# Four edits to a two-layer attention and convolution kernel: an engine for the edge corrections, a queue for two weights, the place of the next image's statistics, and the adder of one block

## The chip, the cores and the metric

The kernel runs on one core of a Trainium2 chip. The core has a matrix engine (TensorE, called PE in the profile), two engines for elementwise work (VectorE, DVE, and ScalarE, ACT), a general one (GpSimd, POOL) and an engine that only issues transfers (SyncE, SP). Each engine works through its own list of instructions in order; semaphores tie the lists together. Loads and stores are DMA transfers, issued by an instruction on SP, POOL or ACT and carried out by 16 DMA engines that all of them share. The metric is the time of the whole program in microseconds of device time; lower is better.

## The reference

The input x has two images of 256 channels and 64 x 64 positions, in fp32. Two layers are applied, each as x + layer(GroupNorm(x)), with 32 groups in the norm:

```python
# layer 0: 1x1 convolution to q, k, v; 8 heads of 32 channels; all 4096 positions
qkv = einsum('bchw,oc->bohw', gn(x), qkv_w) + qkv_b
x = x + einsum('bhij,bhcj->bhci', softmax(q_i . k_j / sqrt(32)), v)
# layer 1: three 1x1 convolutions of g = gn(x), a position term added to q and k
ctx   = attention over 64 positions, a position from each 8 x 8 block   ("lr")
feats = relu(scale * lr_W(ctx) + shift)
qx, kx = two 1x1 convolutions with scale, shift and relu each, of feats
ctx2  = attention over the 64 positions inside one block, v = sr_fv(feats) ("sr")
out_att  = relu(scale * sr_W(ctx2) + shift)
out_conv = 3x3 grouped convolution, padded by 1, of a mix of q, k and v
x = x + rate1 * out_att + rate2 * out_conv
```

Inside one image everything of layer 1 depends on the statistics of all of layer 0's result. The two images don't depend on each other.

## The kernel before, in words

`direct_layers` handles the images one after the other. x is kept in SBUF as eight tiles of 512 positions (128 partitions, two channel halves each); the pool of them (`xpool`, line 48) has nine places, so eight for an image and one more: a tile of the next image can be loaded when a tile of this one has been released by its last reader.

*Start.* SP's queue holds, in this order, 16 loads of 32 x 256 values into `w1_by_out` and `w2_by_out` (lines 79 to 88), which `fold_scores` (lines 186 to 225) multiplies into weights that layer 1 uses; two small tables; and the eight tiles of x (`load_x`, lines 66 to 74). POOL's queue has the weights of layer 0 (`load_layer0`, lines 120 to 131) and many small constants. `group_stats` (line 331) takes the statistics of x tile by tile on DVE, sums them over the channel groups by two small matmuls, `pm` and `pv`, copies between them on DVE, and ends in a square root on ACT, which needs another table of functions, and a reciprocal on DVE. Then `normalise` makes `xn`, and `project0` (line 392) makes keys (`p_wk`), queries (`p_wq`) and values, splits keys and queries into high and low halves and stores all of them to DRAM; the attention fetches them head by head.

*Layer 0.* `attention0` works on 16 groups `g` (8 heads, each with two halves of the queries) of 32 blocks `j` of 128 keys. A block has four units of 128 keys x 512 queries. PE makes scores in rounds of 3 + 2 + 2 units (`sa`, `sb`, `sc`, line 493), ACT takes the exponential of each (line 499) into a ring of 28 places, of which 17 lie in a tile `es` and 11 in a tile called `v` (`RING`, line 445), and PE multiplies them with the values (`av`, line 509), some rounds behind. The softmax also needs the sum of each row's exponentials, over all blocks. `add_rows` (line 524) makes it: DVE adds most blocks into a tile `e` (lines 538 to 546, two adds of 128 x 1024 a block), but the seven blocks of `SUMMED` (line 447) are summed by DMAs that POOL issues in `add_in_memory` (lines 548 to 556). The first of the seven, block 3, is copied into `acc` and `pair` (line 554); the other six are added there by accumulating DMAs (line 556). A place of the ring can be written again when both the matmuls and the adds have read it. In a group's first block after the last, DVE adds `acc` and `pair` to `e`, and a matmul with ones makes the row sums. The order of PE, ACT and DVE in this stage is written out by hand (`tc.manual_schedule`).

*Layer 1, first part.* `layer1_first` normalises into groups and runs the "lr" attention; its names end in `_lr`.

*Layer 1, second part.* `layer1_second` (line 1204) goes over eight tiles `t` of 512 positions. For each, PE runs the branches fq and fk (`branch`: matmuls `phq`, `prq`, `phk`, `prk`, with the relu on ACT into `hq`, `rq`, `hk`, `rk`), then `group_attention`, a generator that stops at each `yield`: values (`pvs`) and scores (`sp_sr`); transposes (`at_sr`) and, on DVE, copies into `bd` (line 1043); the products with the values (`pc_sr`, line 1052), which ACT turns into `res_sr` (line 1063). Beside that runs the convolution: POOL transforms the image (`conv_transform`, lines 911 and 915), PE multiplies (`conv_step`, `mm`, line 925) into the one accumulator of the pool `pacc`, ACT copies a part of it to `z`, DVE combines the rest and adds the result into x (lines 934 to 953). The transform is right inside the image; at its borders `conv_edges` (lines 954 to 971) adds or takes away a bias in single columns, rows and corners of x, 88 tiny instructions in all. In image 0, after tile 1, `conv_weights` makes the convolution's weights on DVE piece by piece and stores them; the load of `wf` brings them back and 64 transposes (`pw`, line 884) turn them. At the end of a tile, results that are complete are given out: two `scalar_tensor_tensor` on DVE make rate1 * res + x (line 1322), SP stores them, and with that the tile of x is free. In this part PE's order is written out by hand; the order of the other engines is set by the scheduler.

*Between the images.* The loop (lines 1330 to 1353) starts the next image by `load_x(1)`, `load_layer0(1)` and `group_stats`, after all of `layer1_second(0)`.

Of the kernel before, what the change touches and what calls it, by code (L numbers as in the profile page):

```python
# [12 lines left out]
AF = mybir.ActivationFunctionType  # L13
ALU = mybir.AluOpType
# [3 lines left out]
P = 128  # L18
B, C, H, W = 2, 256, 64, 64
N = H * W  # L20
T = 512
NT = N // T
KC = C // P
# [17 lines left out]
def direct_layers(ctx: ExitStack, tc: tile.TileContext, a: dict, out: bass.AP, bad: bass.AP):  # L41
# [24 lines left out]
    def load_x(b):  # L66
        tiles = []
        for t in range(NT):
            xt = xpool.tile([P, KC, T], F32, tag="x", name=f"x_{b}_{t}")
            nc.sync.dma_start(  # L70
                out=xt,
                in_=a["x"][b, :, t * T : (t + 1) * T].rearrange("(k p) n -> p k n", p=P),
            )
            tiles.append(xt)
        return tiles
# [4 lines left out]
    for name in ("w1", "w2"):  # L80
        by_out[name] = wpool.tile([P, KC, C], F32, tag="wp", name=f"{name}_by_out")

        for i in range(4):
            for half in range(2):
                r = 64 * (i % 2) + 32 * half
                nc.sync.dma_start(
                    out=by_out[name][r : r + 32, i // 2, :], in_=a["wx"][int(name == "w2"), half, i, 0:P:4, :]
                )
    place_rows = w4([4, C], "place_rows")
    nc.sync.dma_start(out=place_rows, in_=a["posq"])  # L90
    grid = const.tile([2, 64], F32, name="grid")
# [239 lines left out]
    def group_stats(xts, tagn):  # L331
        st = Stats(xts, tagn)
        for t in range(NT):
            for k in range(KC):
                st.tile(k, t)
        both, pv = slice(0, KC), bank([P, KC], f"pv_{tagn}")
        st.aggregate(both)
        st.means(both, bank([P, KC], f"pm_{tagn}"), nc.vector.tensor_copy)
        st.spread(both)
        st.variances(both, pv)  # L340
        st.deviations(both, pv)
        return st.mean, st.rstd
# [103 lines left out]

    SUMMED = (3, 7, 11, 15, 18, 22, 26)


    SUMMED_LAST = (NJ - 3, NJ - 2, NJ - 1)  # L450

    def attention0(b, xts, held):
# [71 lines left out]
        def add_rows(g, j):  # L524
            if j == 0:
                sums[g] = psum["sc"].tile([P, T], F32, tag="av", name=f"av_{b}_{g}")
                added[g] = [w4([P, 2, T], f"e_{b}_{g}_{w}") for w in range(2)]
                return
            for w in range(2):
                dst = added[g][w]  # L530
                if j in SUMMED:
                    if w == 0:
                        add_in_memory(g, j)
                    continue
                if j == 1:
                    first = two_units(g, 0, w), two_units(g, 1, w)
                    if len(first[0]) == len(first[1]) == 1:
                        nc.vector.tensor_add(dst, first[0][0][1], first[1][0][1])
                    else:
                        for s in range(2):  # L540
                            nc.vector.tensor_add(dst[:, s, :], unit(g, 0, 2 * w + s), unit(g, 1, 2 * w + s))
                    continue
                for s, src in two_units(g, j, w):
                    if g == last and j in SUMMED_LAST:
                        continue
                    nc.vector.tensor_add(dst[:, s, :], dst[:, s, :], src)  # L546

        def add_in_memory(g, j):
            assert not waiting or j != SUMMED[0]
            runs = [(acc[u].unsqueeze(1), unit(g, j, u).unsqueeze(1)) for u in (0, 1)]  # L550
            runs += [(pair[:, s, :], src) for s, src in two_units(g, j, 1)]
            for dst, src in runs:
                if j == SUMMED[0]:
                    nc.gpsimd.dma_start(out=dst, in_=src)
                else:
                    nc.gpsimd.dma_start(out=dst, in_=src, accum_op=ALU.add)  # L556
# [397 lines left out]
    def conv_edges(xts, t):  # L954

        btap, edges = kept["bias"]
        for m in range(2):
            def add(dst, what):
                nc.vector.tensor_scalar(dst, dst, what, None, ALU.add)

            x = xts[t][:, m, :]
            add(x[:, 0:T:W], edges[:, m, 3:4])
            add(x[:, W - 1 : T : W], edges[:, m, 4:5])
            if t == 0:
                add(x[:, 0:W], edges[:, m, 1:2])
                add(x[:, 0:1], btap[:, m, 0:1])
                add(x[:, W - 1 : W], btap[:, m, 2:3])
            if t == NT - 1:
                add(x[:, T - W : T], edges[:, m, 2:3])
                add(x[:, T - W : T - W + 1], btap[:, m, 6:7])  # L970
                add(x[:, T - 1 : T], btap[:, m, 8:9])
# [229 lines left out]
        kept["seam"] = done.ins  # L1201
        return feats, mean, rstd, shift

    def layer1_second(b, xts, feats, mean, rstd, shift, pacc):

        xp = apool.tile([P, KC, PADW, PADW], F32, tag="A", name=f"xp_{b}")
        for k in range(KC):
# [24 lines left out]
        def conv():  # L1232
            nonlocal done, wf
            if wf is None:
                wf = fetch_conv_weights(b)
            if done + 1 < len(turns):
                ahead[done + 1] = conv_transform(b, xp, *turns[done + 1])
            conv_step(b, xts, wf, ahead.pop(done), *turns[done], pacc)
            done += 1

        if b:
            for t in range(3):
# [3 lines left out]
        for t in range(NT):  # L1246
# [25 lines left out]
            with tc.manual_schedule(engines={mybir.EngineType.PE}):  # L1272
                q = branch("fq1", "fq2", V_FQ1, V_FQ2, "q")
                if pending:
                    next(pending)
                    next(pending, None)
                    pending = None
                for tt in images.get(t, ()):
                    to_image(tt)
                if 0 in spots.get(t, ()):  # L1280
                    conv()
                k = branch("fk1", "fk2", V_FK1, V_FK2, "k")
                res = w4([P, KC, T], f"res_{nt}")

                def to_res(m, pc, res=res):

                    bn_relu(
                        res[:, m, :].rearrange("p (d o e) -> p o d e", d=8, o=8),
                        pc.rearrange("p (o d e) -> p o d e", o=8, d=8), V_SRW, m,
                    )  # L1290

                parts = group_attention(
                    nt, q, k, lambda c, w, f=f: f[c][:, w * P : (w + 1) * P], wts["fv"], to_res, apart=t + 1 < NT
                )
                next(parts)
                if 1 in spots.get(t, ()):
                    conv()
                if t < 2 and b == 0:
                    pending = parts
                else:  # L1300
                    next(parts)
                    next(parts, None)
                if 2 in spots.get(t, ()):
                    conv()
# [12 lines left out]
                report()  # L1317
            results[t] = res
            for n in sorted(n for n in results if done >= 4 * (n // 2 + 1)):
                res = results.pop(n)  # L1320
                for m in range(KC):
                    nc.vector.scalar_tensor_tensor(  # L1322
                        res[:, m, :], res[:, m, :], wts["rate1"], xts[n][:, m, :], ALU.mult, ALU.add
                    )
                nc.sync.dma_start(
                    out=out[b, :, n * T : (n + 1) * T].rearrange("(k p) n -> p k n", p=P), in_=res
                )


    for b in range(B):  # L1330
        xts = x_first if b == 0 else load_x(b)
        w0 = w0_first if b == 0 else load_layer0(b)
        with tc.tile_pool(name=f"ps0_{b}", bufs=8, space=PSUM) as psum["ps"]:
            if b == 0:
                fold_scores()
            mean, rstd = group_stats(xts, f"l0_{b}")
            xn = apool.tile([P, KC, N], F32, tag="A", name=f"xn_{b}")
            for t in range(NT):
                for k in range(KC):
                    normalise(xn[:, k, t * T : (t + 1) * T], xts[t][:, k, :], k, mean, rstd)  # L1340
            held = project0(b, xn, w0)
        if b == 0:
            load_layer1()
        load_set(b, ("w3",) if b == 0 else ("g", "w3"))
        with tc.tile_pool(name=f"sc_{b}", bufs=1, space=PSUM) as psum["sc"]:
            put, check, st = attention0(b, xts, held)
        with tc.tile_pool(name=f"ps1_{b}", bufs=8, space=PSUM) as psum["ps"]:
            between = layer1_first(b, xts, put, check, st)
        with (
            tc.tile_pool(name=f"pacc_{b}", bufs=1, space=PSUM) as pacc,  # L1350
            tc.tile_pool(name=f"ps2_{b}", bufs=4, space=PSUM) as psum["ps"],
        ):
            layer1_second(b, xts, *between, pacc)


@with_exitstack
# [555 lines left out]
```

## Time and profile before

| | |
|---|---|
| median of 3 runs | 3140.06 us (3138.55 to 3142.82) |
| the profiled execution, its own time | 3143.21 us |
| its span, first to last instruction | 3141.1 us |
| mean granted clock of PE | 0.992 |

Span and busy time by stage, in us, as read from the trace:

| stage | from, to | PE busy | DVE busy | ACT busy | DMA share |
|---|---|---|---|---|---|
| start: loads and statistics | 0 to 32.0 | 9.4 | 12.2 | 5.3 | 0.78 |
| image 0, projections | 32.0 to 118.0 | 84.4 | 36.1 | 26.8 | 0.82 |
| image 0, layer 0's attention | 118.0 to 1177.0 | 1046.0 | 962.3 | 982.3 | 0.79 |
| image 0, layer 1, first part | 1177.0 to 1281.0 | 99.6 | 92.7 | 45.6 | 0.20 |
| image 0, layer 1, second part, and the change of images | 1281.0 to 1597.0 | 292.0 | 202.9 | 98.2 | 0.18 |
| image 1, projections | 1597.0 to 1683.0 | 85.1 | 35.5 | 26.7 | 0.77 |
| image 1, layer 0's attention | 1683.0 to 2741.0 | 1040.1 | 960.0 | 979.1 | 0.80 |
| image 1, layer 1, first part | 2741.0 to 2846.0 | 100.5 | 36.2 | 43.5 | 0.07 |
| image 1, layer 1, second part | 2846.0 to 3141.1 | 280.7 | 146.1 | 91.5 | 0.04 |

Busy time counts every stretch in which an engine has an instruction at work. A clock below 1.00 means that the throttle granted PE less than its full speed. In the lists of waits, a line names an instruction, what released it, the total idle time, how often, and the longest. In the lines of the timeline stand the start, the duration, the engine, the source line, the operation, its output and inputs, how many instructions are taken together (x...), and in brackets the idle time of the engine before the first of them with what ended it. SPq and POOL mark the issue of a transfer, not the transfer.

### The profile page before, as it was taken

The page shows a single profiled execution, that of the slowest core. Times are in us where ns is not written, and L with a number is a line of the kernel's source. Part 1 is how long each engine was busy: PE and PEld are TensorE (multiplying, and loading weights), DVE is VectorE, ACT ScalarE, POOL GpSimd, SP SyncE. Part 2 cuts the span into 40 slices and gives each one's busy share as a digit, 9 for nine tenths or more (in the row PEclk, how much of TensorE's full clock was granted, in tenths as well). Part 3 has the DMA queues.
Part 4 walks back from the last instruction along what each step waited for, and adds up shares of the span by engine and source line. Part 5 has one row for each costly group of instructions (what it writes and reads, how often), then busy time and mean ns, then how long its engine had stood idle before and what let it go on. Part 6 is the DMA issues. An engine that isn't in the chain of part 4 may idle for free. (4 is left out here: it accounts for less than half of the span.)

```text
span 3141.1 us, 62513 instructions
## 1 busy us (share of the span) xinstructions
PE 3037.7 (97%) x25049; PEld 1831.2 (58%) x25049; DVE 2484.0 (79%) x3205; ACT 2298.8 (73%) x2352; POOL 849.5 (27%) x945
## 2 busy tenths in 40 slices
PE   7999999999999999899988999999999999899998
PEld 4455555555555556576754555555555555466765
DVE  4599989999899989946545899889999899835543
ACT  2599999999999983522225999999999999834232
POOL 3022222222223230145401222222222222305440
PEclk9999999999999999999999999999999999999999
DMA  7969779787897661320159696797978975700000
GB/s 246 267 133 183 142 155 168 155 177 151 168 181 159 126 142 31 98 100 33 41 181 264 131 184 142 153 173 147 176 156 168 179 160 118 179 4 4 21 14 22
DMA packets 242729, 426.48 MB, mean 136 GB/s; under 512 B 99080, under 2 KB 109884, under 8 KB 239996
## 3 DMA queue, kind: packets, MB, share of 16 engines
q0 software_dynamic: 96368, 240.46, 39.9%
q1 hardware_dynamic: 146060, 181.94, 21.5%
q8 instruction: 198, 3.24, 0.4%
q14 instruction: 103, 0.84, 0.1%
HBM read 119.03 MB, written 68.39 MB: 60 GB/s over the span
## 5 line engine op out<-in xcount | busy, mean ns | idle before, releaser
L546 DVE TENSOR_TENSOR e<-e,es 128x1024 f32<-128x1024 f32 (+1 forms) x952 | 1034.8, 1142 | 91.2 <-ACT es L499 89.5
L509 PE MATMUL av<-es,v 128*32 128x256 f32 (+1 forms) x9644 | 748.2, 391 | 0.0
L546 DVE TENSOR_TENSOR e<-e,v 128x1024 f32<-128x1024 f32 (+1 forms) x640 | 675.7, 1108 | 52.8 <-ACT v L499 51.7
L499 ACT ACTIVATE es<-sa 128x1536 f32<-128x1536 f32 (+1 forms) x444 | 636.2, 1433 | 101.0 <-PE sa L493 55.8
L493 PE MATMUL sa<-q,k 128*128 128x512 f32 x1736 | 561.2, 430 | 14.3 <-ACT es L499 6.9
L509 PE MATMUL av<-v 128*32 128x256 f32 (+1 forms) x6228 | 506.5, 389 | 0.0
L509 PEld LDWEIGHTS av<-es,v 128*32 128x32 f32 x9644 | 316.5, 109 | 300.8 <-issue 162.8
L493 PEld LDWEIGHTS sa<-q,k 128*128 128x128 f32 x1736 | 280.1, 188 | 297.7 <-issue 134.6
L493 PE MATMUL sc<-q,k 128*128 128x512 f32 x1180 | 371.7, 396 | 7.8 <-ACT es L499 6.3
L493 PE MATMUL sb<-q,k 128*128 128x512 f32 x1180 | 370.8, 395 | 0.0
L509 PEld LDWEIGHTS av<-v 128*32 128x32 f32 x6228 | 216.5, 109 | 178.4 <-issue 81.1
L499 ACT ACTIVATE es<-sc 128x1024 f32<-128x1024 f32 x296 | 306.6, 1036 | 5.8 <-DMA v<-es 5.8
L499 ACT ACTIVATE v<-sc 128x1024 f32<-128x1024 f32 x294 | 304.6, 1036 | 0.3 <-DMA acc<-v 0.3
L499 ACT ACTIVATE es<-sb 128x1024 f32<-128x1024 f32 x296 | 302.3, 1021 | 1.3 <-DMA acc<-es 1.3
L499 ACT ACTIVATE v<-sb 128x1024 f32<-128x1024 f32 x294 | 300.2, 1021 | 0.9 <-DMA acc<-v 0.9
L493 PEld LDWEIGHTS sc<-q,k 128*128 128x128 f32 x1180 | 210.1, 188 | 80.2 <-ACT es L499 19.8
L493 PEld LDWEIGHTS sb<-q,k 128*128 128x128 f32 x1180 | 221.0, 188 | 54.3 <-ACT es L499 1.4
L499 ACT ACTIVATE v<-sa 128x1536 f32<-128x1536 f32 (+1 forms) x146 | 209.3, 1434 | 35.8 <-PE sa L493 14.0
L925 PE MATMUL mm<-v,wf 128*128 128x256 f32 x1024 | 230.2, 383 | 4.5 <-DVE z L934 4.5
L556 POOL DMA_DIRECT2D es<-es x118 | 101.0, 856 | 466.5 <-ACT es L499 414.8
L925 PEld LDWEIGHTS mm<-v,wf 128*128 128x128 f32 x1024 | 195.1, 192 | 40.7 <-issue 12.7
L915 POOL TENSOR_TENSOR v<-col 128x512 f32<-128x512 f32 x128 | 165.7, 1319 | 196.1 <-DVE x L946 44.1
(261 smaller groups left out, 3192.8 us busy)
## 6 DMA issues: line engine op xcount, KB each, us to landing
acc<-es POOLq DMA_DIRECT2D x130, 512.0 KB, 6.4
acc<-v POOLq DMA_DIRECT2D x84, 512.0 KB, 6.3
es<-es POOLq DMA_DIRECT2D x138, 256.0 KB, 4.3
v<-es POOLq DMA_DIRECT2D x134, 256.0 KB, 5.0
k<-wk_halves SPq DMA_DIRECT2D x64, 512.0 KB
q<-wq_halves SPq DMA_DIRECT2D x256, 128.0 KB
v<-v POOLq DMA_DIRECT2D x90, 256.0 KB, 5.3
es<-v POOLq DMA_DIRECT2D x86, 256.0 KB, 4.0
```

What stands on the lines that cost most here:

```text
L493: nc.tensor.matmul(sc[:, i, :], held["k", g // 2][:, j * P : (j + 1) * P], held["q", g, u // 2][:, u % 2, :], start=True, stop=True,)
L499: nc.scalar.activation(dst, sc[:, i : i + m, :], AF.Exp, scale=SC0)
L509: nc.tensor.matmul(dst[HD0 * u : HD0 * u + HD0, n], lhs, rhs(u)[:, n], start=start, stop=stop)
L546: nc.vector.tensor_add(dst[:, s, :], dst[:, s, :], src)
L556: nc.gpsimd.dma_start(out=dst, in_=src, accum_op=ALU.add)
L915: (nc.gpsimd.tensor_add if plus else nc.gpsimd.tensor_sub)(dst, rows(one), rows(two))
L925: nc.tensor.matmul(mm[:, m, r, :], wf[:, k, 4 * r + q, m * P : (m + 1) * P], v[r // 2][:, r % 2, k, :], start=k == 0, stop=k == KC - 1,)
```

## The change

Four edits, all in `direct_layers`:

- The two weights to fold are loaded by eight DMAs of 64 x 256 on ACT's queue, where there were 16 of 32 x 256 on SP's. ACT's instructions of `fold_scores` come behind them.
- In group 0 of each image block 3 is no longer summed by DMA. `summed(g)` leaves it out; DVE adds it, and block 7 becomes the first of six, the one that is copied and not added.
- In image 0's last tile the results that are still outstanding are given out before the branch fk, by a new function `give`, which holds the code that stood at the end of the loop. After the transposes of the last tile's attention, and before its `pc_sr`, comes `following()`: the next image's loads of x and of layer 0's weights, and its statistics. In PE's order `pm` and `pv` of image 1 thus stand ahead of the last `pc_sr`, and in ACT's the table load and the square root ahead of the last two `res_sr`.
- The 88 edge corrections become activations (Identity with a bias) on ACT instead of `tensor_scalar` on DVE. Where they stand in ACT's order is up to the scheduler: those of x's tiles 0, 1, 2 and a part of 4 all come in tile 0 of image 0's second part, ahead of `rq`, `hk`, `rk` and the exponential there; others stand ahead of a copy to `z` or around `rq` and `rk`; in image 1 ten stand ahead of `rq` of tile 1, and the others ahead of `z` or `rk`, `hq` of later tiles.

```diff
--- before.py
+++ after.py
@@ -81,11 +81,11 @@
         by_out[name] = wpool.tile([P, KC, C], F32, tag="wp", name=f"{name}_by_out")
 
         for i in range(4):
-            for half in range(2):
-                r = 64 * (i % 2) + 32 * half
-                nc.sync.dma_start(
-                    out=by_out[name][r : r + 32, i // 2, :], in_=a["wx"][int(name == "w2"), half, i, 0:P:4, :]
-                )
+            r = 64 * (i % 2)
+            nc.scalar.dma_start(
+                out=by_out[name][r : r + 64, i // 2, :],
+                in_=a["wx"][int(name == "w2"), :, i, 0:P:4, :],
+            )
     place_rows = w4([4, C], "place_rows")
     nc.sync.dma_start(out=place_rows, in_=a["posq"])
     grid = const.tile([2, 64], F32, name="grid")
@@ -446,6 +446,11 @@
 
     SUMMED = (3, 7, 11, 15, 18, 22, 26)
 
+    def summed(g):
+
+        return SUMMED if g else SUMMED[1:]
+
+
 
     SUMMED_LAST = (NJ - 3, NJ - 2, NJ - 1)
 
@@ -528,7 +533,7 @@
                 return
             for w in range(2):
                 dst = added[g][w]
-                if j in SUMMED:
+                if j in summed(g):
                     if w == 0:
                         add_in_memory(g, j)
                     continue
@@ -546,11 +551,11 @@
                     nc.vector.tensor_add(dst[:, s, :], dst[:, s, :], src)
 
         def add_in_memory(g, j):
-            assert not waiting or j != SUMMED[0]
+            assert not waiting or j != summed(g)[0]
             runs = [(acc[u].unsqueeze(1), unit(g, j, u).unsqueeze(1)) for u in (0, 1)]
             runs += [(pair[:, s, :], src) for s, src in two_units(g, j, 1)]
             for dst, src in runs:
-                if j == SUMMED[0]:
+                if j == summed(g)[0]:
                     nc.gpsimd.dma_start(out=dst, in_=src)
                 else:
                     nc.gpsimd.dma_start(out=dst, in_=src, accum_op=ALU.add)
@@ -956,7 +961,7 @@
         btap, edges = kept["bias"]
         for m in range(2):
             def add(dst, what):
-                nc.vector.tensor_scalar(dst, dst, what, None, ALU.add)
+                nc.scalar.activation(dst, dst, AF.Identity, bias=what)
 
             x = xts[t][:, m, :]
             add(x[:, 0:T:W], edges[:, m, 3:4])
@@ -1201,7 +1206,7 @@
         kept["seam"] = done.ins
         return feats, mean, rstd, shift
 
-    def layer1_second(b, xts, feats, mean, rstd, shift, pacc):
+    def layer1_second(b, xts, feats, mean, rstd, shift, pacc, following):
 
         xp = apool.tile([P, KC, PADW, PADW], F32, tag="A", name=f"xp_{b}")
         for k in range(KC):
@@ -1237,6 +1242,14 @@
                 ahead[done + 1] = conv_transform(b, xp, *turns[done + 1])
             conv_step(b, xts, wf, ahead.pop(done), *turns[done], pacc)
             done += 1
+
+        def give(n):
+            res = results.pop(n)
+            for m in range(KC):
+                nc.vector.scalar_tensor_tensor(
+                    res[:, m, :], res[:, m, :], wts["rate1"], xts[n][:, m, :], ALU.mult, ALU.add
+                )
+            nc.sync.dma_start(out=out[b, :, n * T : (n + 1) * T].rearrange("(k p) n -> p k n", p=P), in_=res)
 
         if b:
             for t in range(3):
@@ -1279,6 +1292,9 @@
                     to_image(tt)
                 if 0 in spots.get(t, ()):
                     conv()
+                if b == 0 and t == NT - 1:
+                    for n in sorted(results):
+                        give(n)
                 k = branch("fk1", "fk2", V_FK1, V_FK2, "k")
                 res = w4([P, KC, T], f"res_{nt}")
 
@@ -1299,6 +1315,8 @@
                     pending = parts
                 else:
                     next(parts)
+                    if b == 0 and t == NT - 1:
+                        following()
                     next(parts, None)
                 if 2 in spots.get(t, ()):
                     conv()
@@ -1317,23 +1335,22 @@
                 report()
             results[t] = res
             for n in sorted(n for n in results if done >= 4 * (n // 2 + 1)):
-                res = results.pop(n)
-                for m in range(KC):
-                    nc.vector.scalar_tensor_tensor(
-                        res[:, m, :], res[:, m, :], wts["rate1"], xts[n][:, m, :], ALU.mult, ALU.add
-                    )
-                nc.sync.dma_start(
-                    out=out[b, :, n * T : (n + 1) * T].rearrange("(k p) n -> p k n", p=P), in_=res
-                )
-
+                give(n)
+
+
+    ahead = {}
+
+    def following():
+        xts = load_x(1)
+        ahead.update(xts=xts, w0=load_layer0(1), stats=group_stats(xts, "l0_1"))
 
     for b in range(B):
-        xts = x_first if b == 0 else load_x(b)
-        w0 = w0_first if b == 0 else load_layer0(b)
+        xts = x_first if b == 0 else ahead["xts"]
+        w0 = w0_first if b == 0 else ahead["w0"]
         with tc.tile_pool(name=f"ps0_{b}", bufs=8, space=PSUM) as psum["ps"]:
             if b == 0:
                 fold_scores()
-            mean, rstd = group_stats(xts, f"l0_{b}")
+            mean, rstd = group_stats(xts, "l0_0") if b == 0 else ahead["stats"]
             xn = apool.tile([P, KC, N], F32, tag="A", name=f"xn_{b}")
             for t in range(NT):
                 for k in range(KC):
@@ -1350,7 +1367,7 @@
             tc.tile_pool(name=f"pacc_{b}", bufs=1, space=PSUM) as pacc,
             tc.tile_pool(name=f"ps2_{b}", bufs=4, space=PSUM) as psum["ps"],
         ):
-            layer1_second(b, xts, *between, pacc)
+            layer1_second(b, xts, *between, pacc, following)
 
 
 @with_exitstack
```

## The prediction

> **What bounds the kernel now.** I read the page's first two parts, then the list of who PE waited for, then the timeline around each long wait. The page says that PE is the floor:
>
> ```profile
> PE 3037.7 (97%) x25049; PEld 1831.2 (58%) x25049; DVE 2484.0 (79%) x3205; ACT 2298.8 (73%) x2352; POOL 849.5 (27%) x945
> PE   7999999999999999899988999999999999899998
> ```
>
> About 103 us of the 3141.1 us span are without a matmul, and slices 0, 16, 20, 21, 34 and 39 hold them. Only there can this change pay. PE's waits (total us, times, longest) name the causes:
>
> ```profile
> PE pm_l L315 <- DVE mv_l L312: 18.7, 3, 9.6
> PE pc_sr L1052 <- DVE bd L1043: 11.6, 3, 6.7
> PE sa L493 <- ACT es L499: 6.9, 4, 4.5
> PE sc L493 <- ACT es L499: 6.3, 7, 3.8
> PE pw L884 <- DMA wf<-wf_kept: 2.8, 1, 2.8
> ```
>
> The timeline (start, duration, engine) of the first 32 us: SP issues 16 small loads before any of x, and DVE's statistics wait for x.
>
> ```profile
> 0.74 7.37 SPq L86 DMA_DIRECT2D w_by_out<-in_wx_dram  x16
> 8.84 5.36 SPq L70 DMA_DIRECT2D x<-in_x_dram  x8
> 23.14 5.23 DVE L308 BATCH_NORM_STATS2 stats_l<-x 128x6 f32<-128x512 f32 x8 [1.93 <-DMA x<-in_x_dram]
> 32.07 15.45 PE L400 MATMUL p_wk<-xn,wqk 128*128 128x512 f32 x32 [1.14 <-DVE xn L350]
> ```
>
> In the first group of each image, ACT's exponential wants ring slots that block 3 still holds for a slow copy by DMA:
>
> ```profile
> 127.32 0.53 POOL L554 DMA_DIRECT2D acc<-es  x1 [0.27 <-ACT es L499]
> 142.17 1.02 ACT L499 ACTIVATE es<-sc 128x1024 f32<-128x1024 f32 x1 [3.98 <-DMA v<-es]
> ...
> 1693.37 0.54 POOL L554 DMA_DIRECT2D acc<-es  x1
> 1712.44 1.45 ACT L499 ACTIVATE es<-sa 128x1536 f32<-128x1536 f32 x1 [5.67 <-DMA acc<-es]
> ```
>
> Between the images, and at the convolution's weights in image 0:
>
> ```profile
> 1581.17 0.42 SPq L70 DMA_DIRECT2D x<-in_x_dram  x1
> 1594.48 1.28 ACT L328 ACT_TABLE_LOAD   x1 [2.08 <-PE pv_l L325]
> 1596.94 16.36 PE L400 MATMUL p_wk<-xn,wqk 128*128 128x512 f32 x32 [2.54 <-DVE xn L350]
> ...
> 1325.87 9.29 DVE L959 TENSOR_SCALAR x<-x,edges 128x8 f32<-128x8 f32 x9
> 1335.07 0.85 DVE L1043 COPY bd<-at_sr 64x256 f32<-64x256 f32 x2
> 1342.29 8.84 PE L884 MATMUL pw<-ident,wf 128*128 128x128 f32 x64 [2.85 <-DMA wf<-wf_kept]
> ```
>
> [...] the edge corrections last 227 ns in the median, but up to 2168 ns from 1325.87 on, where GpSimd's 2.14 us and 1.2 us operations run. [...] 0.83 granted at 140 to 150 us and 0.50 at 1333 to 1338 us. [...]
>
> **A. Weights to fold on ACT's queue.** Removed from SP: 16 issues, 7.37 us. Placed ahead on ACT: 8 issues. ACT's issue is not in the trace; SP's 0.46 us and POOL's 0.49 us (3.95 us for 8) bracket it, so some 4 us. SP's first x load should start at 0.74 + (8.84 - 8.15) = 1.4 us instead of 8.84, a shift of 7.4 us. Does x then land as much earlier? From 10 to 26 us the DMA share was 0.93 to 1.09 and 4.9 MB passed: x (4.19 MB) and layer 0's weights (0.78 MB). So landing is bound by the rate, some 309 GB/s. Now the 0.52 MB to fold compete with x, up to 1.7 us; against that the layer 0 weights, issued by POOL at 10.9 as before, compete with only its last part. I take 0.4 us off: **-7.0 us**, between -4.5 and -8.5. What is late next? Layer 0's keys' weights landed at 18.3 us, and the first p_wk would be at 25: covered. ACT's fold chain (9.84 to 19.3 us, 9.5 us) would start near 6 and end near 16, while pm_l, behind it on PE, is due at 22: 6 us of cover. From 32 us to the attention PE is fed without a gap, so the shift goes through whole.
>
> **B. Block 3 of the first group on DVE.** Per image: three DMAs of 1 MB leave POOL's queue, and DVE gets two adds of 128x1024 (1217 ns each, 2.4 us). Rounds of scores (sa to sa) take some 3.4 us once settled. In image 0 one round took 138.03 to 147.21 = 9.2 us and another 4.3: 6.7 us too many. In image 1: 10.15 and 4.8: 8.1 us, part of it slow clock behind the gap. Is DVE's addition covered? From 122.5 to 193.4 us DVE worked 58.5 us and idled 12; with 2.4 more it ends near 184 if never starved, and the row sums on PE that read it come 6.2 us after its last add now (193.45 to 199.65). Covered. What is late next is block 7, now the first copy, whose slots are wanted at the round of units 56 to 58. In image 0 that is 119.2 + 8 rounds = 146 us; it can be issued at 134 to 135.5, and the same megabyte of block 3 had landed by 144. In image 1: due 1685 + 27 = 1712, and 1712.4 is when block 3's last copy landed, on the same load of queries, keys and values. So almost in time; I leave 0.7 and 1.1 us of stall: **-6.0 and -7.0 us**. Bounds: -14.8 if no stall is left; -6 if block 7 keeps half of it. Below that it cannot go, as each later block is one link shorter behind.
>
> **C. Statistics amid the last tile.** Tile 6's result no longer has edge corrections between its two scalar_tensor_tensor (1578.14 and 1579.89): it ends 1.1 us earlier, so the last x load goes at 1580.0 and, with the same 6.2 us, lands at 1586.2. DVE: two statistics 1.3, the value copy 0.65, two bd copies 0.85, aggregation 0.6: ready at 1589.6. From aggregation to the end of the square root the first image shows 28.86 to 30.34 (pv_l), and this switch 1594.01 to 1596.03: 3.5 us. So 1593.1. PE's pc_sr (2.0 us) runs within that, where it stood ahead of pm_l before. Then p_wk waits for ACT's two res_sr (1.6 us), now queued behind the square root: 1594.8 against 1596.94, **-2.1 us**. Moved along: x and weight loads by SP and POOL keep their order, so nothing is passed there; the wait new on PE is pc_sr's behind pv_l, hidden in the same interval. Bounds: -0.5 [...] and -3.3.
>
> **D. Edge corrections on ACT.** DVE loses 88 instructions (27.0 + 3.7 + 2.5 = 33.2 us); [...] At 1325.87 nine corrections stand ahead of bd, and PE idles 6.7 us. That wait goes: bd could follow at 1327.7, and pc_sr end at 1332. But the stall stays: pw needs wf, whose load SP issued at 1328.44, after the last made weight, and which landed at 1342.3. Only the 7 corrections inside the making of the weights (0.14 us each, 1 us) bring it earlier[...]. Value **0**, bounds -1.5 and +1.5. Elsewhere PE hardly waits for DVE, so relief is worth nothing. New on ACT's in-order queue are corrections that wait for DVE's additions ahead of rk_sr in tiles 2, 4 and 6 of image 1 (rk_sr 2953.0, four corrections from 2952.8, sp_sr due 2955.4) and ahead of two z copies: **+0.8 us**, bounds 0 and +3.
>
> **Sum.** -7.0 - 13.0 - 2.1 + 0 + 0.8 = -21.3 us. The profiled execution took 3143.21 us (span 3141.1), so 3121.9; it stood 3.15 above the median 3140.06, so the median to expect is **3118.8**.
>
> **Rivals.**
> 1. Block 7 takes over the stall: POOL's copies still lie behind keys and values (19 us to land at 1693). Half of B is lost: 3118.8 + 6.5 = 3125.3. For: the share of DMA stays at 1.0 until 1745; against: it is issued some 8 us later, and block 3's own megabyte is no longer in front of it.
> 2. x lands no earlier than the rate allows, with the fold weights in between: A gives 2.5: 3123.3. For: shares above 0.93 from 10 us; against: 0.26 to 0.39 from 2 to 10 us, which is room.
> 3. The weights' stall shrinks with its blocked corrections, wf being earlier by some 4 us: 3114.8. Against: SP's order above.
> 4. The other side: ACT's queue. A correction waiting for DVE holds z or rk_sr behind it, and PE then waits for the accumulator that z empties. There are 14 such places in the two images; at 1.5 us each the gain is eaten (21.3 / 14), at 3 us the time is 3140 + 21 = 3161. Against: in the timeline DVE's additions end before ACT's next due instruction in all but a few, and PE has 7 us of convolution there.
>
> **Chances.** Forecast 0.60 (own range 3113 to 3124), rival 1 0.18, rival 2 0.09, rival 3 0.08, rival 4 0.05, of which 0.03 slower. A difference of 0.2%, 6.3 us, is about what a measurement of this kernel can tell from no change. So faster 0.95, same 0.02, slower 0.03. The range takes in rivals 1 to 3 and the bounds: 3109 to 3130.
>
> **What would show it.** SP's x at 1.4 us and first p_wk near 25; no exponential waiting for a DMA over 1.5 us before 200 us, and DVE adding through; p_wk of image 1 some 2 us sooner after the last x issue; bd at once behind at_sr at the weights, and pw's wait for wf grown to 9 us. Wrong would be: block 7's acc landing after its slots are wanted; sp_sr or mm waiting for ACT more than 0.5 us often; pw starting more than 1.5 us from its place relative to the last wf_kept store.

## The result, and the profile after

The changed kernel takes 3130.03 us in the median of 7 runs (3126.40 to 3134.51), the kernel before 3142.40 us in 7 runs made beside them: ratio 0.9964, 95% interval 0.9953 to 0.9976. By the medians it is 12.4 us faster, where I had forecast 21.3. The ratio is taken over the runs and not from the two medians, so here and below the two can differ by 1 to 2 us; the interval is the ratio's. The profiled execution of the changed kernel took 3126.40 us with a span of 3124.2 us. It is the fastest of its seven, so the two profiles lie 16.9 us apart, more than the medians.

PE's share of the span is what it was, 97%. The list of who PE waited for (engine, line, tile, what ended the wait: total us, times, longest us), of the kernel after:

```profile
PE pt_g L206 <- issue: 11.5, 1, 11.5
PE pm_l L315 <- DVE mv_l L312: 11.1, 3, 6.8
PE pt_meet L206 <- ACT query_part L202: 10.3, 1, 10.3
PE pw L889 <- DMA wf<-wf_kept: 10.2, 1, 10.2
...
PE pc_sr L1057 <- DVE bd L1048: 1.9, 2, 1.5
...
PE sa L498 <- ACT es L504: 1.9, 2, 0.9
```

Two of the old waits have shrunk as the forecast said: `sa` for the exponential from 6.9 to 1.9 us, and `pc_sr` for `bd` from 11.6 to 1.9. The wait of `pw` for the load of `wf` has grown from 2.8 to 10.2, which is the stall that the forecast said would stay. The top is new: `pt_g`, the product of the two weights to fold, waited 11.5 us. The timeline of the first 40 us of the kernel after (start, duration, engine):

```profile
0.73 10.23 ACTq L85 DMA_DIRECT2D w_by_out<-in_wx_dram  x8
...
1.49 14.85 SPq L70 DMA_DIRECT2D x<-in_x_dram  x8
...
17.76 1.29 DVE L308 BATCH_NORM_STATS2 stats_l<-x 128x6 f32<-128x512 f32 x2 [7.18 <-DMA x<-in_x_dram]
...
28.09 1.19 PE L206 MATMUL pt_g<-w_by_out 128*128 128x256 f32 x2 [11.46 <-issue]
...
37.18 3.61 PE L400 MATMUL p_wk<-xn,wqk 128*128 128x512 f32 x4 [1.13 <-DVE xn L350]
```

SP's first load of x is issued at 1.49 us, as forecast. But the eight issues then take 14.85 us instead of 5.36, DVE stands still for 7.18 us before the third tile of x, the weights to fold are complete only at 28 us, and the first `p_wk` comes at 37.2 us, where it came at 32.1 and was forecast for 25.

Where the time went, by the start of single matmuls in the two profiled executions (us):

| | before | after | shift |
|---|---|---|---|
| first `p_wk`, image 0 | 32.1 | 37.2 | +5.1 |
| first scores | 117.9 | 123.2 | +5.3 |
| first row sums | 199.6 | 199.5 | -0.1 |
| first `phq_sr`, image 0 | 1281.5 | 1281.3 | -0.2 |
| first `pw` | 1342.3 | 1341.3 | -1.0 |
| first `p_wk`, image 1 | 1596.9 | 1591.2 | -5.7 |
| first scores, image 1 | 1683.7 | 1675.6 | -8.1 |
| first row sums, image 1 | 1767.0 | 1752.7 | -14.3 |
| last `pc_sr` starts | 3129.9 | 3115.2 | -14.7 |

So the first edit lost 5 us where it should have won 7, the second won 5.4 and 6.2, and the change of images won 4.7 and then 2.4 more in the projections behind it. From the row sums of image 0 to `phq_sr` the executions of all kernels of this study take 1081.7 to 1084.1 us, and I read nothing into differences of that size there.

### The profile page after: what moved, and what is told of

Read it like the earlier page. It is cut to its first block, busy times and chain, and to the rows that moved or that the text cites. A ratio compares the mean times of both kernels' runs of the same rounds, so it can differ in the third digit from the quotient of the medians.

```text
span 3124.2 us, 62490 instructions
## 1 busy us (share of the span) xinstructions
PE 3030.2 (97%) x25049; PEld 1826.3 (58%) x25049; DVE 2457.5 (79%) x3121; ACT 2315.7 (74%) x2440; POOL 843.4 (27%) x939
## 5 line engine op out<-in xcount | busy, mean ns | idle before, releaser
L551 DVE TENSOR_TENSOR e<-e,es 128x1024 f32<-128x1024 f32 (+1 forms) x956 | 1039.5, 1147 | 77.6 <-ACT es L504 76.3
L498 PEld LDWEIGHTS sc<-q,k 128*128 128x128 f32 x1180 | 209.8, 187 | 75.9 <-ACT es L504 12.3
```

The lines of the kernel that those rows point to most:

```text
L498: nc.tensor.matmul(sc[:, i, :], held["k", g // 2][:, j * P : (j + 1) * P], held["q", g, u // 2][:, u % 2, :], start=True, stop=True,)
```

## The experiments

In each, "before" is measured beside the kernel; I give the medians, the ratio with its interval, and then what the trace shows.

**The first edit alone** (lines 84 to 88 as in the change, nothing else).

> The kernel before with the first edit alone: the two weights to fold loaded on ACT's queue. Theory 1 (two queues of loads hold each other up: in the changed kernel SP's third x load is issued only at 10.98 us, and the first p_wk comes at 37.2 us in place of 32.1): the first p_wk again near 37, everything behind it 5 us later, time +3 to +7 us. Rival (the edit by itself gains as I forecast, and the delay was a matter of that one execution): the first p_wk near 25, time -7 us. Between the two (the rate binds anyway): first p_wk 30 to 33, time 0 to -2.

3148.46 us against 3143.05: ratio 1.0014 (1.0005 to 1.0023), 5.4 us slower by the medians. The first `p_wk` comes at 38.2 us (37.2 in the changed kernel). The loss is the edit's own, and not an accident of one execution.

**The second edit alone** (`summed(g)`).

> The kernel before with the second edit alone: block 3 of group 0 added by DVE. Theory (the stall is gone and block 7's copy is in time): first row-sum matmul of image 0 some 5.5 us earlier and that of image 1 some 6 us earlier relative to the start of its scores; no exponential waits over 1.5 us for a DMA; time -10 to -13 us, with up to 2 us of it given back by short waits later in the attention. Rival 1 of the forecast (block 7 takes over half the stall): -6 us, with a wait of 3 to 4 us on acc or v near block 7.

3130.80 us against 3143.05: ratio 0.9960 (0.9945 to 0.9974), -12.3 us. From the first scores to the first row sums image 0 takes 76.4 us instead of 81.7, image 1 75.4 instead of 83.3. The longest waits of PE for an exponential in these groups are under 1 us. The theory holds, and rival 1 of the forecast falls in this execution. The other traces agree: in the six kernels without this edit the two stretches take 81.3 to 84.5 and 81.9 to 83.5 us, in the eight with it 74.9 to 76.5 and 75.1 to 78.0, but for one of 80.8.

**The third edit alone** (`give` and `following`, edge corrections on DVE).

> The kernel before with the third edit alone: the next image's statistics amid the last tile, the edge corrections still on DVE. Theory (the gain is the order of PE and ACT and the table load that no longer waits): first p_wk of image 1 3 to 4.5 us earlier, and the projections behind it 2 us faster[...]: time -4 to -7 us. Rival (the gain needs the edge corrections off DVE, since they hold the results that free x's tile): p_wk only 1 to 2 us earlier, time -1 to -3.

3137.81 us against 3143.05: ratio 0.9990 (0.9983 to 0.9998), -5.2 us by the medians and -3.1 by the ratio. From `pw` to the first `p_wk` of image 1 it takes 250.1 us instead of 254.6. The edge corrections, still on DVE, lie behind the two `scalar_tensor_tensor` here and don't hold them, so the rival falls. One part of the theory fell too: the projections behind, from `p_wk` to the scores, took 86.5 us (86.8 before). Over the 20 us from the first `p_wk` the granted clock was 0.89 (0.88 in the kernel before), and the last `pc_sr` took 3.76 us (2.02 there):

```profile
1586.30 3.76 PE L1052 MATMUL pc_sr<-bd,vs_sr 128*128 128x128 f32 x16
```

**The fourth edit alone** (edge corrections on ACT).

> The kernel before with the fourth edit alone: the 88 edge corrections on ACT. Theory (the wait in front of bd goes, but the load of wf ends the wait of pw as before, about 1 us earlier): pw's wait for wf grows to some 10 us, first pw 1 to 2 us earlier, time 0 to -3 us. Rival 4 of the forecast (ACT's queue holds z and rk behind corrections): +2 to +10 us, with sp_sr and mm waiting for ACT in many tiles of the second part.

3139.45 us against 3143.05: ratio 0.9991 (0.9982 to 0.9999), -3.6 us by the medians and -2.8 by the ratio. PE's wait for `wf` grew to 9.9 us and the first `pw` came 0.9 us earlier, where 1 to 2 were expected. That 0.9 us can't be told from the spread: from `phq_sr` to `pw` the kernels without this edit take 59.1 to 61.0 us, those with it 59.6 to 60.1. The rest was won at the change of images: from `pw` to `p_wk` 251.7 us instead of 254.6. No wait of `sp_sr` or `mm` for ACT grew: rival 4 falls.

**The eight wide loads, but on SP's queue**: is it the queue or the shape?

```diff
-            for half in range(2):
-                r = 64 * (i % 2) + 32 * half
-                nc.sync.dma_start(
-                    out=by_out[name][r : r + 32, i // 2, :], in_=a["wx"][int(name == "w2"), half, i, 0:P:4, :]
-                )
+            r = 64 * (i % 2)
+            nc.sync.dma_start(
+                out=by_out[name][r : r + 64, i // 2, :],
+                in_=a["wx"][int(name == "w2"), :, i, 0:P:4, :],
+            )
```

> The kernel before, the weights to fold loaded by eight DMAs of 64 x 256 as in the change, but on SP's queue ahead of x as before. Theory 1 (it is the second queue that costs: SP's loads of x and ACT's loads hold each other up): issue of the eight takes 3.5 to 5 us, x starts at 4.5 to 6 us, first p_wk 2 to 3 us earlier than before (29 to 30), time -2 to -3 us. Theory 2 (the shape of 64 rows costs, on whichever queue: in the changed kernel 48 rows a us passed, in the one before 70): the eight take about 10 us to issue, x starts at 11 us, first p_wk at 34 to 36, time +2 to +4 us.

3147.57 us against 3142.93: ratio 1.0019 (1.0010 to 1.0027), +4.6 us. The eight issues took 7.19 us, not 10, and x started at 9.64, only 0.8 us later than before; but the first `p_wk` came at 37.4, 5.3 us later. So the loss is in the landing, and it is there with one queue alone: theory 2, the shape.

**The sixteen narrow loads, but on ACT's queue** (`nc.sync` becomes `nc.scalar`, lines 86 to 88).

> The kernel before, the sixteen loads of 32 x 256 unchanged but on ACT's queue. Theory 1 (the second queue costs): SP's loads of x stall behind them as in the changed kernel, first p_wk at 35 to 39, time +3 to +7 us. Theory 2 (the shape costs): no stall of SP, x landed by 22 us, first p_wk at 25 to 29, time -3 to -7 us.

3138.84 us against 3142.93: ratio 0.9984 (0.9977 to 0.9991), -4.1 us; the first `p_wk` comes at 28.0. This is theory 2 again: with narrow loads the second queue gains. How the shape costs is seen in the DMA traffic of the first us. The same stretches (length, busy of PE, PEld, DVE, ACT, POOL with instructions, granted clock, DMA share, GB/s), first of the kernel after and then of this one:

```profile
2.00:6.00 4.00, 0.37 (x2) 0.29 (x2) 0.00 (x0) 0.00 (x0) 3.90 (x9) 1.00 0.78 230
6.00:10.00 4.00, 0.00 (x0) 0.00 (x0) 2.00 (x4) 0.00 (x0) 1.98 (x5) 1.00 0.32 101
```

```profile
2.00:6.00 4.00, 0.37 (x2) 0.29 (x2) 0.40 (x1) 0.00 (x0) 3.90 (x9) 1.00 0.84 267
6.00:10.00 4.00, 0.00 (x0) 0.00 (x0) 2.17 (x4) 0.00 (x0) 2.31 (x6) 1.00 1.04 250
```

From 6 to 10 us the 16 DMA engines of the kernel after lie idle for two thirds, while x is wanted. From 8 to 12 us their share is 0.16, so on average 2.6 of them have work, and they move 49 GB/s. The totals of ACT's queue (packets, MB, share of 16 engines) tell why, first after, then this one:

```profile
q10 hardware_dynamic: 528, 0.52, 0.1%
```

```profile
q10 hardware_dynamic: 768, 0.53, 0.1%
```

Both moved 512 rows of 1 KB, so 512 packets of data. What is over are packets of 4 bytes, 16 for eight loads and 256 for sixteen. I read them as one report from each engine that took part in a load; then each wide load was done by 2 engines and each narrow one by 16. That is a reading, for the trace doesn't name a packet's engine. But it has the packets' times: in the kernel after, the 512 rows of the weights pass from 2.2 to 27.4 us, and for 96% of that time no more than two of them are under way at once.

**The wide loads, taken row by row.** The source of a wide load is two halves of 32 rows, halves outermost. Here the rows are outermost; loads, queue and bytes are those of the changed kernel. Two small copies turn a table to match.

```diff
-                in_=a["wx"][int(name == "w2"), :, i, 0:P:4, :],
+                in_=a["wx"][int(name == "w2"), :, i, 0:P:4, :].rearrange("h r c -> r h c"),
...
+        turned_rows = w4([4, KC, 2, 32, 2], "turned_rows")
+        for h in range(2):
+            nc.scalar.copy(
+                turned_rows[:, :, :, :, h], place_rows.rearrange("q (k a h r) -> q k a h r", k=KC, a=2, h=2)[:, :, :, h, :]
+            )
...
```

> The changed kernel with the same eight loads of 64 x 256 on ACT's queue, but each load's source taken row by row (32 rows, each with its two halves) and no longer half by half (two halves of 32 rows); the rows of both weights lie in that order, and the small table is turned to match by two tiny copies on ACT. Theory 3 (the eight loads were served by two of the sixteen DMA engines, for the trace shows 16 completion packets of 4 bytes for eight loads where the sixteen narrow loads have 256; with 32 outermost they spread over all): 128 completion packets, no lull of the DMA share between 6 and 12 us, first p_wk at 26 to 29 us in place of 37.2, time -8 to -11 us against the changed kernel. Rival (a load of 64 rows is slow whatever its order): first p_wk at 35 to 39, time as the changed kernel.

3123.71 us against 3143.40: ratio 0.9936 (0.9922 to 0.9949), -19.7 us, where the changed kernel has -12.4. That is a gain of 7 to 9 us over the changed kernel, by the medians or by the ratios; 8 to 11 were expected. Its totals of ACT's queue:

```profile
q10 hardware_dynamic: 640, 0.52, 0.1%
```

That makes 128 reports, 16 for each load. The statistics of x are complete at 20.7 us (28.3 before), the DMA share from 6 to 12 us is 0.83 (0.27 in the changed kernel), and theory 3 holds. But the shape is not all: SP's issues of x took 10.71 us for nine here, though by the packets no load ran on two engines, 10.46 for nine in the next kernel, and 12.15 for eight with the narrow loads on ACT's queue. In the kernel before, with nothing on ACT's queue, eight took 5.36. So with loads on a second queue x's issues took longer in any shape; with the wide ones, by the packets on two engines, they took longest, 14.85 us for eight. The first `p_wk` at 27.5 was still 2.5 us late, and the timeline of ACT names the reason:

```profile
24.62 0.17 ACT L231 COPY w_at<-pt_g 128x5 f32<-128x5 f32 x1 [8.80 <-POOL w_at L184]
...
26.44 0.26 ACT L335 ACTIVATE rstd_l<-pv_l,eps 128x2 f32<-128x2 f32 x1
```

The scheduler had put a copy into `w_at` ahead of the square root (`rstd_l`), and it waited for POOL's clearing of `w_at`, which stands behind POOL's loads.

**The same, with `w_at` cleared by DVE at the start.**

> The kernel with rows outermost (all four edits, the eight loads on ACT's queue spread over all DMA engines), in which the square root still waited 4 us behind a copy into w_at that waited for POOL's clearing of it at 24.4 us. Here DVE clears w_at at the very start. If the loads over two engines were the whole of what went wrong with the first edit: statistics complete at 20.7 us again, the square root at once behind pv_l, first p_wk at 24 to 25 us in place of 32.1 before (the -7 us of my forecast), and the time 2 to 4 us below the last kernel's 3123.7: 3120 to 3122. If layer 0's weights, whose loads POOL issues from 14.5 us on, become the wait: first p_wk at 26 to 28, time 3123.

3121.58 us against 3141.63: ratio 0.9933 (0.9919 to 0.9946), -20.1 us. The timeline of its first 30 us:

```profile
20.66 0.58 DVE L319 BATCH_NORM_AGGREGATE mv_l<-stats_l 128x2 f32<-128x48 f32 x2
...
23.35 0.26 ACT L335 ACTIVATE rstd_l<-pv_l,eps 128x2 f32<-128x2 f32 x1 [2.64 <-PE pv_l L332]
...
25.18 11.09 PE L407 MATMUL p_wk<-xn,wqk 128*128 128x512 f32 x19 [1.87 <-DVE xn L357]
```

The first `p_wk` comes 6.9 us earlier than before, at the 25 us that the forecast had for the changed kernel, and from 7 to 11 us the packets of ACT's queue took 27.1% of the time of 16 engines, so of 4.3 engines in the mean (10.3%, so 1.6, in the changed kernel). The whole time shows only a part of that: 3121.58 us against 3125.16 for the next kernel, which has the old loads. In the trace of this one image 1 loses some 3 us in its first group and 3 at the change of images and behind it, both taken up below.

**The change without its first edit.**

> The changed kernel without its first edit: the weights to fold on SP's queue as before, the other three edits made. If the edits add up: first p_wk at 32.1 again, everything behind it as in the changed kernel, 5 to 6 us faster than that: some 3122 us, -20 us against before. If the stall in image 0 comes back as the attention now starts earlier (its DMAs collide with other loads), only 2 us of it are kept.

3125.16 us against 3142.93: ratio 0.9940 (0.9928 to 0.9953), -17.8 us, so 5 us better than the changed kernel. The stalls in the first group did not come back: from scores to row sums it takes 75.8 and 77.6 us, in the changed kernel 76.3 and 77.1.

**The second and third edit without the fourth.**

> The kernel before with the second and the third edit: block 3 on DVE and the early statistics, without the loads on ACT's queue and with the edge corrections on DVE. If the third and the fourth edit took the same wait at the change of images (each alone -3.6 to -5.2 us by the medians, both together -5.5), the fourth is worth 0 to -2 us beside the third, and this kernel takes 3125 to 3128 us. If their gains are separate, it is 3 to 4 us slower than the kernel with both: 3129.

3126.32 us against 3143.40: ratio 0.9946 (0.9932 to 0.9959), -17.1 us. The fourth edit adds 0.7 us by the medians and 1.9 by the ratios, less than these can tell apart; alone it took 3.6 and 2.8. The traces show that third and fourth take in part the same wait. From `pw` to the first scores of image 1 the five kernels without either take 341.4 to 343.5 us, the fourth alone 338.9, the two kernels with the third alone 336.6 and 338.7, the six with both 334.3 to 339.4. In the mean that is 3.4, 4.6 and 5.8 us better than neither, where separate gains would add up to 8.0. Here the last `pc_sr` of image 0 took 3.76 us, in the changed kernel 2.03. The fourth edit doesn't decide that: the two kernels with rows outermost have all four edits, and single matmuls of `pc_sr` up to 561 ns, as here (377 in the changed kernel).

**x first.** Three edits (not the first), and SP's queue turned round, with the fold called behind the statistics; the lines show the difference to the kernel without the first edit.

```diff
+    x_first = load_x(0)
     by_out = {}
...
-    x_first = load_x(0)
...
+            mean, rstd = group_stats(xts, "l0_0") if b == 0 else ahead["stats"]
             if b == 0:
                 fold_scores()
-            mean, rstd = group_stats(xts, "l0_0") if b == 0 else ahead["stats"]
```

> The kernel of the last expectation, with SP's queue turned round: x first, then the sixteen loads of 32 x 256 of the weights to fold, whose matmuls come behind the statistics' on PE. The first x load is issued at 1.5 us, x has landed by 19 to 22 us, first p_wk at 22 to 25 us in place of 32. The matmuls of the fold (some 5 to 10 us) now lie among the projections: the first scores come 2 to 6 us earlier than in the kernel of the last expectation, time -2 to -6 us against it. If the fold's weights land late (after 27 us), PE waits for them behind the first p_wk and nothing is gained.

3118.88 us against 3142.93: ratio 0.9926 (0.9914 to 0.9938), -24.1 us, 6.3 less than with the old order. The first matmul of the statistics (`pm_l`) starts at 18.4 us (28.9 before), the first `p_wk` at 24.7, and the first scores came 6.2 us earlier.

**The same, with block 7 on DVE as well** (`SUMMED[2:]` in group 0).

> The kernel with x first (three edits, weights to fold behind x on SP), and in group 0 block 7 added by DVE too, so that block 11 is the first copy. If block 7's copy still holds ring places (some 3 us of waits of 0.2 to 0.9 us are left in the first groups): -1 to -3 us. If those waits have another cause (the projections' end, exponentials): 0. If DVE, with 2.4 us more in the group, becomes late for the row sums: +1 to +3 us, with a wait of the row-sum matmul for DVE.

3117.74 us against 3143.40: ratio 0.9922 (0.9908 to 0.9936). Against the last kernel that is some 1 us by the ratios, which the intervals don't separate. In the trace a single exponential of the first groups still waits for a DMA, 0.2 us, and from scores to row sums it takes 74.9 and 75.1 us (75.6 and 77.3 with block 7 by DMA). DVE wasn't late. By its median this is the fastest kernel of the study.

## Why the prediction was wrong

**The step that failed is the landing of x in A**: from "SP's first x load should start at 0.74 + (8.84 - 8.15) = 1.4 us instead of 8.84, a shift of 7.4 us" I went on to a landing "bound by the rate", with the bounds -4.5 to -8.5. The first issue was right (1.49 us). The landing wasn't, and neither were the issues behind, of which the third came at 10.98 us: I costed eight loads of twice the rows as half the issues and the same transfer, and never asked on how many DMA engines a load of that form runs. By the packets it ran on two: 16 reports for the eight loads with two halves outermost, 128 for the same eight with 32 rows outermost, 256 for sixteen of 32 rows. Instead of -7.0 the step was worth +5.1 in the trace, +5.4 alone and +4.9 as the difference to the kernel without it. With the rows outermost it was worth -6.9 to the first `p_wk`, and less in the whole time. Loads on two engines can explain the size, by an estimate: 512 rows at 46 ns each (the middle of these packets' times in the trace) are 23.6 us, on two engines 11.8, beside x, if a part of its rows passes these two as well. Why SP's queue stands still while ACT's has loads, though the DMA share from 6 to 12 us is 0.27, I didn't try.

No rival covered it. Rival 2 had the right place (x no earlier), but with a rate as its cause and a gain of 2.5 us as its worst.

**A's cover.** "6 us of cover" for ACT's fold chain failed with the same cause: the chain ended at 34.6 us, behind the statistics, and on PE its last matmuls, which end at 34.2 us, stood ahead of `pm_l`, whose input was ready at 33.1.

**B was right in cause and size**: forecast -6.0 and -7.0, measured -5.4 and -6.2 in the changed kernel, -5.3 and -7.9 alone, -12.3 us by the medians. (Of its bounds, -6 for half of the stall left should have been -7.4, half of 14.8.) The slow clock that the forecast saw behind the gap in image 1 is a granted 0.66 from 1713 to 1718 us of the kernel before. ACT's waits for block 7, for which I left 0.7 and 1.1 us, are there, and a second wait of 1.2 and 1.5 us for `v` some 9 us later. ACT's timeline of the kernel after, in the first group of each image:

```profile
152.09 1.46 ACT L504 ACTIVATE es<-sa 128x1536 f32<-128x1536 f32 x1 [0.73 <-DMA acc<-es]
...
1704.95 1.45 ACT L504 ACTIVATE es<-sa 128x1536 f32<-128x1536 f32 x1 [1.17 <-DMA acc<-es]
```

Rival 1 was not empty, though. In the execution with the mended loads one wait of 2.6 us for a place in `v` stood in image 1, and scores to row sums took 80.8 us there.

**C was right in sign and too small**: -2.1 was forecast, with the bounds -0.5 to -3.3. In the changed kernel's trace it is -4.7 us to `p_wk` and 2.4 more behind it, alone -5.2 us by the medians. Two terms were mis-sized. The last x load landed 4.7 us after its issue, where I kept 6.2. From the end of the aggregation to the end of the square root it took 2.1 us, not 3.5, because the table load (1.28 us) no longer stands in between. And PE's clock was left out. The last wait of `p_wk`, for `res_sr`, is the one that I had forecast. The timeline of the kernel after:

```profile
1583.47 1.28 ACT L328 ACT_TABLE_LOAD   x1
...
1586.83 0.35 PE L315 MATMUL pm_l<-mv_l,group 128*128 128x2 f32 x2 [2.05 <-DVE mv_l L312]
...
1588.33 2.03 PE L1057 MATMUL pc_sr<-bd,vs_sr 128*128 128x128 f32 x16
1588.51 0.26 ACT L328 ACTIVATE rstd_l<-pv_l,eps 128x2 f32<-128x2 f32 x1 [3.75 <-PE pv_l L325]
...
1591.23 9.28 PE L400 MATMUL p_wk<-xn,wqk 128*128 128x512 f32 x21 [0.87 <-ACT res_sr L1068]
```

The table load runs while DVE still has `bd` to copy, and PE's longest gap is 2.05 us. Before, there was one of 3.35 us and three more behind it (0.87, 1.18 and 2.54). The granted clock over the 20 us from the first `p_wk` was 0.88 before and 1.00 after, and 0.12 of 20 us is the 2.4 us. It looks as if a shorter gap paid twice, but the other runs don't bear that out. The third edit alone, and the second and third without the fourth, show the same gap of 2.05 us, and the `pc_sr` behind it took 3.76 us there; in the changed kernel, in that without its first edit and in the one with x first it took 2.03 behind 2.05. Single matmuls of `p_wk` took up to 1219 ns in the former two and 697 in the latter three. The two kernels with rows outermost, which have all four edits, go with the former: up to 1219 and 1222 ns. In the kernel before, `pc_sr` took 2.02 us behind 3.35 us of gap. So one gap was followed by either speed, and a part of what C won in this trace can't be counted on. What decides between the two was not shown.

**D was right at the weights and misplaced elsewhere.** The wait for `bd` went, the wait for `wf` took its place, and `pw` came 1.0 us earlier (bound -1.5). But the 1.1 us that I booked under C, for `scalar_tensor_tensor` no longer interrupted by corrections, belong to either edit: each alone takes them. In the sum, C and D were forecast at -2.1 together and gave -5.5 by the medians (17.8 - 12.3). One correction on ACT lasted 297 ns in the middle (128 x 8). What it holds of ACT's queue is less: 59 corrections that follow another at once start 198 ns after it in the middle. The trace of the kernel before has no correction on ACT, so what the forecast allowed for their time there was an estimate of mine without a measured price.

**ACT's frictions** were forecast at +0.8: image 1's second part, from `phq_sr` to the last `pc_sr`, took 283.4 us before and 283.6 after. The executions of all kernels take 281.8 to 283.6 us there, so no friction is seen.

**The sum.** Forecast -7.0 - 13.0 - 2.1 + 0 + 0.8 = -21.3. By the medians of the parts it is +5.4 - 12.3 - 5.5 = -12.4, and -12.4 was measured. That they agree to a tenth is luck, for each part is known to 3 to 5 us only. A came out 12.4 us worse than forecast (+5.4 for -7.0); C, D and the frictions came out 4.2 us better together, which hid a third of it.

## What to carry to other kernels

Before costing a load that has been made wider, look at the outermost dimension of its source, not only at its size: the same eight loads ran, by their packets, on 2 engines each with 2 outermost (16 reports) and on 16 with 32 outermost (128). In a trace it shows as packets over the data: count them per load. Then look at what shares the time with it: with loads on ACT's queue SP took 1.2 to 1.9 us for each issue of x, in every shape tried, against 0.67 in the kernel before, and the statistics of x were complete soonest with x first on one queue (`pm_l` starts at 18.4 us, and at 21.3 and 21.4 with the rows outermost on the second queue). And when two edits aim at the same wait, forecast that wait once, and don't count on a clock that one profile shows.

## What the runs showed of the hardware

From 8 to 12 us of the kernel after, the DMA engines moved 49 GB/s; 0.18 of these 0.19 MB were the wide loads, by their packets on 2 of 16 engines. SP's eight issues of x took 5.36 us in the kernel before, with nothing on ACT's queue, 12.15 with the sixteen narrow loads there, and 14.85 with the eight wide ones (1.49 to 16.34 us, the third at 10.98). With rows outermost nine issues took 10.71 and 10.46 us.

The kernel before, the second edit alone and the narrow loads on ACT's queue, which lack both the third and the fourth edit, took 6.0 to 6.2 us from the issue of the last x load of image 1 to its statistics; six kernels with either or both took 4.7. In the kernel before, one DMA of the instruction queue, 16 KB, lies inside that load:

```profile
q8 instruction: 1, 0.02, 3.0%
```

That is the total of that queue from 1581.0 to 1584.7 us; from 1585.2 to 1587.2 us, until the load lands, the DMA share is 0.03 to 0.08, so about one of 16 engines is busy. This DMA starts 2.5 us after the load's issue; in the changed kernel one starts 4.2 us after it, and with the fourth edit alone none lies within the first 4 us. That this costs the 1.2 to 1.5 us is argued from the times, not tried.
